# Ten matrix products of the last sequence written into the folding of a batch norm, and a load asked for earlier

## The chip, the cores and the metric

One Trainium2 chip, and one core of it. The metric is the device time of one execution in microseconds, the median of the runs. The engines are named as in the profile: PE (TensorE matmuls), PEld (its weight loads), DVE (VectorE), ACT (ScalarE), POOL (GpSimd) and SP (SyncE, which issues the DMAs here).

## What is computed

A block of two layers over 8 sequences of 512 tokens with 256 features. The change lies in the last of four parts, a product-key layer of experts. Cut to that part:

```python
def _L1_ffn_ref(x, w_q, bn_gamma, bn_beta, keys, down_embed, up_embed):   # x: normalized, (8, 512, 256)
    q = jnp.einsum('bnd,de->bne', x, w_q)                  # 2048 columns
    mean = jnp.mean(q, axis=(0, 1))
    var = jnp.var(q, axis=(0, 1))
    q = (q - mean) * jax.lax.rsqrt(var + BN_EPS) * bn_gamma + bn_beta
    q = q.reshape(b, n, 2, H, KD).transpose(2, 0, 1, 3, 4)
    sim = jnp.einsum('pbnhd,hkpd->pbnhk', q, keys)
    sx, ix = jax.lax.top_k(sim[0], TOPK)
    sy, iy = jax.lax.top_k(sim[1], TOPK)
    all_scores = (sx[..., :, None] + sy[..., None, :]).reshape(b, n, H, TOPK * TOPK)
    all_indices = (ix[..., :, None] * NUM_KEYS + iy[..., None, :]).reshape(b, n, H, TOPK * TOPK)
    scores, pk = jax.lax.top_k(all_scores, TOPK)
    indices = jnp.take_along_axis(all_indices, pk, axis=-1)
    wd = down_embed[indices]
    wu = up_embed[indices]
    h = gelu_new(jnp.einsum('bnd,bnhkd->bnhk', x, wd))
    h = jax.nn.softmax(scores, axis=-1) * h
    return jnp.einsum('bnhk,bnhkd->bnd', h, wu)
```

The three parts before it are a gated recurrence with a matrix memory, a block of attention with experts, and a cross attention. Each part is added to x with a gate.

## The kernel before

**Two phases.** `attention_phase` computes the first three parts for one sequence after another, in the order 0, 4, 1, 5, 2, 6, 3, 7. At the end of each sequence `leave(m)` stores x (`x_d`), the normalized and transposed x (`xT_d`), and adds the sequence's products of x with itself into `gacc` and its sums into `xsum`. `chosen_phase` then computes the experts' part for 32 tiles of 128 tokens.

**The products with down.** The kernel doesn't gather rows of down. It multiplies x with all 4096 rows, sequence by sequence, in `inner_products(m)`, and stores the result in `g_d` in DRAM. A sequence needs 32 products, in 16 pairs. A product is two matmuls (L285), each of two passes in the trace, into a PSUM tile `ps_hd` from a pool of two buffers, and a copy of 128x512 into one half of `raw`, on ACT (L241) or DVE (L243). A planner (`Clock`, `Room`) chooses the copy's engine by counts of its own. A pair needs its 256 KB of down (`dw`, two buffers; the load for the pair after next is asked for right after a pair) and the sequence's x (`dx`, one buffer, 512 KB, loaded once at the start of the sequence). `raw` has two buffers too; a pair's store of 512 KB to `g_d` is issued when the generator is stepped for the next pair. All these DMAs go through SP, by `send` (L138).

**How products are spread.** `inner_products` is a generator, stepped by `down_lane`. In the attention phase a scheduler steps it in between. For the last sequence, m = 7, it has to wait for `leave(7)`, so its 32 products fall in `chosen_phase`, where `late_products(n)` steps the lane until n products are written.

**An order written by hand.** On PE, DVE, ACT, POOL and SP the instructions run in the order in which the program writes them. An instruction that waits holds up whatever is behind it on its engine.

**Between the phases** stands `fold()`, which folds the batch norm into the keys. For each of 16 blocks of columns n it multiplies `wq` with `gacc` (`ps_e`, L1568), multiplies that with `wT` on DVE (`pt`, L1573), copies the mean on ACT (`mu`, L1574) and sums on ACT (L1575). Then come short instructions on DVE for the variance (L1577 to L1579), the inverse root on POOL (`inv_sqrt`, L145 and L146), and on DVE the scaling `s` (L1581), `c` (L1583, L1584) and the scaled keys `ksc` (L1586). Then, for two halves and two blocks k, 8 small products with `wT` each (`ps_w`, L1591), copied to `mat` by ACT (L1595), and for each half 8 products of `c` with the keys (L1599), which become `shift` (L1604, L1605). `ps_e`, `ps_w` and, in the attention phase, `ps_hd` share the two buffers of the pool `ps_m`. After the folding, that pool and the weights' pools are closed, and new pools take their place.

**The tile loop** runs n from -3 to 32 in four steps u. Tile t passes through it as a pipeline:

- `similar` (L1662, L1663): the similarities, from `load_tokens` (L1634, the tile's x, `xt`);
- `search` (L1677, L1679), `rank_sums`, `best_pairs`, `differences`, `chosen`, `rows_of`: the best eight twice over, on DVE and POOL;
- `turn_over` (L1778): three transposes of `mlw` on PE;
- `fetch` (L1796): the tile's `g`, 2 MB, from `g_d`; `activate` (L1800): the gelu on ACT;
- `mark_choices` (L1809 to L1830), `weigh` (`cf`, L1842), `multiply` (L1851);
- `add_up` (`acc`, L1861) and the output (`fin`, L1869), one for each tile.

The steps with n < 0 are a prologue. In it the loop also loads `up_sb` in 8 parts of 512 KB (L1916) and fetches the first three `g`. Two products of the last sequence are written in each of the 8 steps of n = -2 and n = -1, and one at the end of each n from 0 to 15:

```python
                late_products(2 if n > -3 else 0)
            elif u == 3:
                late_products(1)
```

The functions that the diff touches, with the line numbers of the profile:

Of the kernel before, what the change touches and what calls it, by code (L numbers as in the profile page):

```python
# [23 lines left out]
B, S, D = 8, 512, 256  # L24
# [61 lines left out]
def kernel(  # L86
# [28 lines left out]
    ck = Clock()  # L115
# [21 lines left out]
    def send(dst, src, after=0.0):  # L137
        nc.sync.dma_start(dst, src)  # L138
        size = 1
        for n in dst.shape:  # L140
            size *= n
        return ck.sent(size, after)
# [5 lines left out]
    def side(t):  # L148

        return ("side", t)  # L150
# [100 lines left out]
    done = {}  # L251
    dws, dw_there, raw_free = {}, [0.0, 0.0], [0.0, 0.0]

    def inner_products(m):

        b = order[m]
        xt = late.tile([P, NK, S], F32, name="dx")
        there = send(xt, xT_d[:, :, b * S : (b + 1) * S])

        def fetch(i):  # L260
            if i < M * (NJ // 2):
                dws[i] = late.tile([P, NK, 2, P], F32, name="dw", bufs=2)
                j = 2 * (i % (NJ // 2))
                dw_there[i % 2] = send(dws[i], down[:, :, j : j + 2, :])

        def store():
            i, raw, t = kept.pop()
            raw_free[i % 2] = send(
                g_d[NC * b : NC * (b + 1), :, 2 * i : 2 * i + 2, :].rearrange(
                    "c p j s -> p c (j s)"  # L270
                ),
                raw.rearrange("p c j s -> p c (j s)"), t,
            )

        if m == 0:
            fetch(0)
            fetch(1)
        kept = []
        for i in range(NJ // 2):
            yield max(there, dw_there[i % 2], raw_free[i % 2])  # L280
            raw = late.tile([P, NC, 2, P], F32, name="raw", bufs=2)
            for u in range(2):
                ps = Room([P, S], "ps_hd")
                for k in range(NK):
                    nc.tensor.matmul(  # L285
                        ps.tile, dws[m * (NJ // 2) + i][:, k, u, :], xt[:, k, :],
                        start=(k == 0), stop=(k == NK - 1),
                    )
                ps.mm(NK * S * F4)
                t = ps.copy(raw[:, :, u, :], ps.tile.rearrange("p (c s) -> p c s", c=NC))  # L290
                if u == 0:
                    yield 0.0
            kept.append((i, raw, t))
            fetch(m * (NJ // 2) + i + 2)
            yield side(t)
            store()
        done[("down", m)] = ck.pe
# [1229 lines left out]
    def lane3():  # L1527
        for m in range(M):
            yield ("rest", ("left", m))
            yield from inner_products(m)  # L1530

    down_lane = Lane(lane3())
    with tc.manual_schedule(
        engines={
            mybir.EngineType.PE, mybir.EngineType.DVE, mybir.EngineType.Activation,
            mybir.EngineType.Pool, mybir.EngineType.SP,
        }
    ):
        with ExitStack() as phase:
            attention_phase(phase, down_lane)  # L1540
        chosen_phase(ctx, tc, locals())


def chosen_phase(ctx, tc, env):
# [5 lines left out]
    ck, down_lane, inv_sqrt = (env[k] for k in ("ck", "down_lane", "inv_sqrt"))  # L1550
# [3 lines left out]
    mat = xs.tile([P, NK, 1024], F32, name="mat")  # L1554
    shift = xs.tile([P, 1024], F32R, name="shift")

    def fold():

        nc.gpsimd.memset(shift.bitcast(F32), 0.0)
        nc.vector.tensor_reduce(gacc[:, :, D], xsum, AX.X, ALU.add)  # L1560
        n_inv = 1.0 / (NT * P)
        nc.vector.tensor_scalar(gacc, gacc, n_inv, None, ALU.mult)
        e2 = wp.tile([P, 16], F32, name="e2")
        mu = wp.tile([P, 16], F32, name="mu")
        for n in range(16):
            ps = ps_m.tile([P, S], F32, name="ps_e", tag="m")
            for k in range(NK):
                nc.tensor.matmul(  # L1568
                    ps[:, : D + 1], wq[:, k, n * P : (n + 1) * P], gacc[:, k, :],
                    start=(k == 0), stop=(k == NK - 1),  # L1570
                )
            pt = fp.tile([P, D], F32, name="pt")
            nc.vector.tensor_tensor(pt, ps[:, :D], wT[:, n, :], ALU.mult)  # L1573
            nc.scalar.copy(mu[:, n : n + 1], ps[:, D : D + 1])  # L1574
            nc.scalar.activation(pt, pt, AF.Copy, accum_out=e2[:, n : n + 1])  # L1575
        s = wp.tile([P, 16], F32, name="s")
        nc.vector.tensor_tensor(s, mu, mu, ALU.mult)  # L1577
        nc.vector.tensor_tensor(s, e2, s, ALU.subtract)
        nc.vector.tensor_scalar(s, s, 0.0, None, ALU.max)  # L1579
        inv_sqrt(s, s, EPS_LN)  # L1580
        nc.vector.tensor_tensor(s, s, bn_sb[:, 0:16], ALU.mult)  # L1581
        c = wp.tile([P, 16], F32, name="c")
        nc.vector.tensor_tensor(c, mu, s, ALU.mult)  # L1583
        nc.vector.tensor_tensor(c, bn_sb[:, 16:32], c, ALU.subtract)  # L1584
        ks = wp.tile([P, 16, 64], F32, name="ksc")
        nc.vector.tensor_tensor(ks, kT, s.unsqueeze(2).to_broadcast([P, 16, 64]), ALU.mult)  # L1586
        for h in range(2):
            for k in range(NK):
                ps = ps_m.tile([P, 8, 64], F32, name="ps_w", tag="m")
                for i in range(8):  # L1590
                    nc.tensor.matmul(  # L1591
                        ps[:, i, :], wT[:, 8 * h + i, k * P : (k + 1) * P], ks[:, 8 * h + i, :],
                        start=True, stop=True,
                    )
                nc.scalar.copy(mat[:, k, 512 * h : 512 * h + 512], ps.rearrange("p i k -> p (i k)"))  # L1595
            ps = ps_m.tile([P, 8, 64], F32, name="ps_w", tag="m")
            for i in range(8):
                n = 8 * h + i
                nc.tensor.matmul(  # L1599
                    ps[0:1, i, :], c[:, n : n + 1], kT[:, n, :], start=True, stop=True  # L1600
                )
            pr = ps[0:1].rearrange("p i k -> p (i k)")
            hi = shift[0:1, 512 * h : 512 * h + 512]
            nc.scalar.copy(hi, pr)  # L1604
            nc.vector.tensor_tensor(  # L1605
                shift[32:33, 512 * h : 512 * h + 512], pr, hi.bitcast(F32), ALU.subtract
            )
# [24 lines left out]
    def load_tokens(t):  # L1632
        sims[("x", t)] = tk.tile([P, NK, P], F32, name="xt2")
        nc.sync.dma_start(sims[("x", t)], xT_d[:, :, t * P : (t + 1) * P])  # L1634

    load_tokens(0)
    fold()
    env["psum_m"].close()
    env["tail"].close()
# [4 lines left out]
    ps_o = ctx.enter_context(tc.tile_pool(name="ps_o", bufs=1, space=PSUM))  # L1644
    ps_t = ctx.enter_context(tc.tile_pool(name="ps_t", bufs=1, space=PSUM))
    env["home"][:] = [ps_s, "sim"]

    def late_products(n):

        for _ in range(n):  # L1650
            work = ck.work
            while not down_lane.over and ck.work == work:
                down_lane.step()

    def similar(t, half):
        if half == 0:
# [221 lines left out]
    for n in range(-3, NT + 1):  # L1878
        for u in range(4):
# [32 lines left out]
            if n < 0:  # L1912
                i = 4 * (n + 3) + u
                if i < 8:
                    at = slice(4 * i, 4 * i + 4)
                    nc.sync.dma_start(up_sb[:, at], up[:, at])  # L1916
                if i in (0, 5, 8):
                    fetch(len(gts))
# [3 lines that stand above are left out]
# [54 lines left out]
```

## Time and profile before

| | us |
|---|---|
| median of 3 runs | 3795.7 |
| lowest and highest run | 3791.03, 3797.01 |
| the profiled execution, its own time | 3808.9 |
| its span, first to last instruction | 3807.1 |
| end of the attention phase (last sum into `gacc`, start) | 2790.82 |
| first `ps_e` on PE | 2793.27 |
| first `ps_w` on PE | 2815.39 |
| first similarity on PE | 2834.48 |
| first product of the last sequence on PE | 2844.21 |
| first output `fin` on DVE | 2946.52 |
| last product of the last sequence on PE, start | 3341.0 |
| last output `fin` on DVE | 3803.94 |

| engine | busy us | share of the span |
|---|---|---|
| PE | 3582.4 | 94% |
| DVE | 2393.4 | 63% |
| ACT | 1706.5 | 45% |
| POOL | 742.8 | 20% |

The mean clock that was granted to TensorE is 0.952 of full speed. SP's queue between the two phases, and in the prologue, issues in this order (start in us): the store of `xT_d` at 2787.61; `xt` of tile 0 at 2790.70; one part of up at 2791.40; `g` of tile 0 at 2809.73, when the weights' pools were free; `xt` of tile 1 at 2810.12; four parts of up from 2810.69; `dx` at 2813.62; and the first `dw` of the prologue at 2847.94.

A row of the timeline or of the windows reads as follows. A timeline row has start, duration, engine, line, operation, output and inputs, shape and count, and in brackets the idle time before it and what ended that. A windows row has the stretch, its length, the busy time of PE, PEld, DVE, ACT and POOL with the number of instructions in brackets, the granted clock, the share of the DMA engines and GB/s.

### The profile page before, as it was taken

What the parts mean: (1) busy time and instruction counts of PE and PEld (TensorE: products, weight loads), DVE (VectorE), ACT (ScalarE), POOL (GpSimd) and SP (SyncE); (2) the same over time, 40 slices, a digit from 0 to 9 for tenths busy, and PEclk for the clock granted to TensorE, in tenths of its full rate; (3) what the DMA queues carried; (4) which work ended last, traced back from release to release, by engine and by line L of the source; (5) the groups of instructions that cost most, each with busy time, mean ns of one, the idle gap of its engine ahead of it and who ended that gap; (6) DMA issues with size and microseconds to landing.
All of it is one profiled execution on the core that took longest, in us unless ns stands there. A gap on an engine that the chain in (4) does not pass through costs nothing. (4 is left out here: it accounts for less than half of the span.)

```text
span 3807.1 us, 61425 instructions
## 1 busy us (share of the span) xinstructions
PE 3582.4 (94%) x24381; PEld 2005.4 (53%) x24381; DVE 2393.4 (63%) x5622; ACT 1706.5 (45%) x2383; POOL 742.8 (20%) x964
## 2 busy tenths in 40 slices
PE   9899999999999999999999999999988999998998
PEld 5544445444544544444444454355354777776777
DVE  4566466565565465556555545443337999999996
ACT  3154555454555554554555454544423333332331
POOL 2011001001001011010000101000024555555544
PEclk9799999899999999999999999998988999999999
DMA  3213213224234225223413433424333323222221
GB/s 106 89 45 122 70 56 135 70 90 147 91 104 166 79 88 165 96 94 118 161 55 112 158 106 119 135 68 135 100 125 123 113 91 122 92 85 106 80 79 58
DMA packets 235264, 395.16 MB, mean 104 GB/s; under 512 B 14048, under 2 KB 167936, under 8 KB 230624
## 3 DMA queue, kind: packets, MB, share of 16 engines
q1 hardware_dynamic: 232080, 388.83, 30.5%
q8 instruction: 192, 3.15, 0.3%
q10 hardware_dynamic: 2896, 2.40, 0.2%
q14 instruction: 96, 0.79, 0.1%
HBM read 252.62 MB, written 138.56 MB: 103 GB/s over the span
## 5 line engine op out<-in xcount | busy, mean ns | idle before, releaser
L724 DVE TENSOR_REDUCE nm<-sc 128x2 f32<-128x1024 f32 x768 | 937.7, 1222 | 795.8 <-PE sc L704 793.0
L762 ACT ACTIVATE pr<-sc 128x1024 f32<-128x1024 f32 x512 | 522.7, 1023 | 504.2 <-PE sc L704 495.7
L285 PE MATMUL ps_hd<-dx,dw 128*128 128x512 f32 x1024 | 515.0, 628 | 5.3 <-DVE pd L1003 2.4
L704 PE MATMUL sc<-ks,qs 32*128 32x512 f32 x1536 | 428.0, 523 | 62.2 <-DVE nm L724 35.2
L1861 PE MATMUL acc<-up_sb,g 128*128 128x256 f32 x2048 | 474.9, 386 | 5.6 <-DVE g L1851 3.9
L1861 PEld LDWEIGHTS acc<-up_sb,g 128*128 128x128 f32 x2048 | 380.1, 190 | 67.6 <-issue 15.8
L765 ACT ACTIVATE pr<-sc,m_off 128x1024 f32<-128x1024 f32 x256 | 283.2, 1112 | 290.2 <-PE sc L704 289.8
L704 PEld LDWEIGHTS sc<-ks,qs 32*128 32x128 f32 x1536 | 164.0, 190 | 454.1 <-issue 228.2
L704 PE MATMUL sc<-qs,ks 32*128 32x512 f32 x1536 | 388.6, 511 | 6.5 <-ACT pr L765 2.7
L1830 POOL TENSOR_TENSOR m<-m2b,wr 64x512 bf16<-64x512 bf16 x256 | 271.6, 1061 | 409.0 <-DVE m L1822 394.9
L704 PE MATMUL sc<-mx,pick_g 4*128 4x512 f32 x1536 | 309.0, 403 | 0.0
L285 PEld LDWEIGHTS ps_hd<-dx,dw 128*128 128x128 f32 x1024 | 180.9, 194 | 219.2 <-issue 191.0
L781 PE MATMUL av<-pr,va 128*32 128x512 f32 x2048 | 288.7, 637 | 2.3 <-ACT pr L762 2.3
L241 ACT COPY raw<-ps_hd 128x512 f32<-128x512 f32 x209 | 122.2, 586 | 295.3 <-PE ps_hd L285 287.0
L1800 ACT ACTIVATE g<-g 128x1024 f32<-128x1024 f32 x128 | 135.3, 1060 | 259.6 <-DMA g<-g_d 217.6
L1842 PEld LDWEIGHTS <-m 128*128 128x128 bf16 x6144 | 208.0, 98 | 36.3 <-issue 21.5
L1842 PE MATMUL cf<-m,m 128*128 128x64 bf16 x6144 | 212.8, 194 | 13.7 <-POOL m L1830 10.7
L970 POOL TENSOR_SCALAR_AFFINE_SELECT mb<-mb 128x256 f32<-128x256 f32 x116 | 47.2, 407 | 908.0 <-ACT pd L979 471.6
L348 PE MATMUL ps_up<-ones,ident 128*128 128x128 f32 x1144 | 209.2, 324 | 6.8 <-DVE dx L906 1.5
L348 PEld LDWEIGHTS ps_up<-ones,ident 128*128 128x128 f32 x1144 | 169.1, 207 | 84.0 <-issue 49.4
L145 POOL TENSOR_SCALAR ln_rs<-ln_mv 128x4 f32<-128x4 f32 x40 | 9.2, 230 | 973.9 <-DVE ln_mv L163 973.9
L1822 DVE TENSOR_TENSOR m<-m2b,wr 64x1024 bf16<-64x1024 bf16 x256 | 178.8, 699 | 8.4
(272 smaller groups left out, 5456.1 us busy)
## 6 DMA issues: line engine op xcount, KB each, us to landing
g_d<-raw SPq DMA_DIRECT2D x128, 512.0 KB
g<-g_d SPq DMA_DIRECT2D x32, 2048.0 KB
dw<-in_down SPq DMA_DIRECT2D x128, 256.0 KB
w1e<-in_w SPq DMA_DIRECT2D x32, 512.0 KB
w2e<-in_w SPq DMA_DIRECT2D x32, 512.0 KB
qs<-im_Aq SPq DMA_DIRECT2D x32, 512.0 KB
ks<-im_Ak SPq DMA_DIRECT2D x32, 512.0 KB
mb<-nM_d SPq DMA_DIRECT2D x29, 512.0 KB
```

The source lines that it names most:

```text
L285: nc.tensor.matmul(ps.tile, dws[m * (NJ // 2) + i][:, k, u, :], xt[:, k, :], start=(k == 0), stop=(k == NK - 1),)
L348: nc.tensor.matmul(ps.tile[:, :P], ident, ones, start=True, stop=True)
L704: nc.tensor.matmul(sc[:, i, :], lhs[r : r + rows], rhs[r : r + rows], start=(n == 0), stop=(n == len(terms) - 1),)
L724: nc.vector.tensor_reduce(self.nm[:, c, 2 * half : 2 * half + 2, g], sc, AX.X, ALU.max, negate=True)
L762: nc.scalar.activation(self.pr[jj], sc, AF.Exp, scale=self.scale)
L765: nc.scalar.activation(self.pr[jj], sc, AF.Exp, bias=m_off[:, col : col + 1], scale=self.scale,)
L781: nc.tensor.matmul(self.av[32 * j : 32 * j + 32, :], self.va[:, c, h * (self.hd + 1) : h * (self.hd + 1) + 32], pr[j // 2][:, j % 2, :], s ...
L1800: nc.scalar.activation(part, part, AF.Gelu_apprx_tanh)
L1822: last = nc.vector.tensor_tensor(m2[r, 0:2, :, NJ * d : NJ * d + NJ, :], m2b[r].unsqueeze(1).to_broadcast([64, 2, 8, NJ, 2]), wr[r, u, 0:2 ...
L1830: after(nc.gpsimd.tensor_tensor(m2[r, 2, :, NJ * d : NJ * d + NJ, :], m2b[r], wr[r, u, 2].unsqueeze(2).to_broadcast([64, 8, NJ, 2]), ALU.mult,
L1842: nc.tensor.matmul(cf[:, s, :], m1[:, s // 2, :, s % 2], m2[:, i, s // 2, :, s % 2], start=(i == 0), stop=(i == 2),)
L1861: nc.tensor.matmul(accs[t], gts[t][:, j, :], up_sb[:, j, :], start=(j == 0), stop=(j == NJ - 1))
```

## The change

`inner_products` notes in `done[("begun", m)]` that its x was asked for. Before `load_tokens(0)` and the folding, the lane is now stepped until the last sequence has begun, so its request for `dx` is written right behind the stores of the attention phase. `late_products` is unchanged, but stands ahead of `fold()`, which now calls it: for one product after each of the blocks n = 7, 10 and 13, for three after the inverse root has been written and before `s` is scaled, and for one after each of the four copies of `mat`. That makes ten. These are the sequence's first ten products (five pairs), with the loads of `dw` and the stores that go with them; the later calls of `late_products` are the same, so the 8 steps of the prologue write the next 16, and the last 6 follow in n = 0 to 5.

```diff
@@ -256,6 +256,7 @@
         b = order[m]
         xt = late.tile([P, NK, S], F32, name="dx")
         there = send(xt, xT_d[:, :, b * S : (b + 1) * S])
+        done[("begun", m)] = there
 
         def fetch(i):
             if i < M * (NJ // 2):
@@ -1554,6 +1555,13 @@
     mat = xs.tile([P, NK, 1024], F32, name="mat")
     shift = xs.tile([P, 1024], F32R, name="shift")
 
+    def late_products(n):
+
+        for _ in range(n):
+            work = ck.work
+            while not down_lane.over and ck.work == work:
+                down_lane.step()
+
     def fold():
 
         nc.gpsimd.memset(shift.bitcast(F32), 0.0)
@@ -1573,11 +1581,14 @@
             nc.vector.tensor_tensor(pt, ps[:, :D], wT[:, n, :], ALU.mult)
             nc.scalar.copy(mu[:, n : n + 1], ps[:, D : D + 1])
             nc.scalar.activation(pt, pt, AF.Copy, accum_out=e2[:, n : n + 1])
+            if n in (7, 10, 13):
+                late_products(1)
         s = wp.tile([P, 16], F32, name="s")
         nc.vector.tensor_tensor(s, mu, mu, ALU.mult)
         nc.vector.tensor_tensor(s, e2, s, ALU.subtract)
         nc.vector.tensor_scalar(s, s, 0.0, None, ALU.max)
         inv_sqrt(s, s, EPS_LN)
+        late_products(3)
         nc.vector.tensor_tensor(s, s, bn_sb[:, 0:16], ALU.mult)
         c = wp.tile([P, 16], F32, name="c")
         nc.vector.tensor_tensor(c, mu, s, ALU.mult)
@@ -1593,6 +1604,7 @@
                         start=True, stop=True,
                     )
                 nc.scalar.copy(mat[:, k, 512 * h : 512 * h + 512], ps.rearrange("p i k -> p (i k)"))
+                late_products(1)
             ps = ps_m.tile([P, 8, 64], F32, name="ps_w", tag="m")
             for i in range(8):
                 n = 8 * h + i
@@ -1633,6 +1645,8 @@
         sims[("x", t)] = tk.tile([P, NK, P], F32, name="xt2")
         nc.sync.dma_start(sims[("x", t)], xT_d[:, :, t * P : (t + 1) * P])
 
+    while ("begun", B - 1) not in env["done"]:
+        down_lane.step()
     load_tokens(0)
     fold()
     env["psum_m"].close()
@@ -1644,13 +1658,6 @@
     ps_o = ctx.enter_context(tc.tile_pool(name="ps_o", bufs=1, space=PSUM))
     ps_t = ctx.enter_context(tc.tile_pool(name="ps_t", bufs=1, space=PSUM))
     env["home"][:] = [ps_s, "sim"]
-
-    def late_products(n):
-
-        for _ in range(n):
...
```

## The prediction

> **What bounds the kernel now.** I read the page first, then the last thousand microseconds in windows, then the timeline of the folding, of the start of the tile loop and of SP's queue. The change touches only what follows 2790 us of a span of 3807.1, so the page's totals (PE 94%) say little here; stages do. The table by windows (span, PE, PEld, DVE, ACT, POOL busy, granted clock, DMA share, GB/s):
>
> ```profile
> 2805.00:2810.00 5.00, 3.57 (x16) 2.40 (x14) 2.38 (x8) 2.84 (x16) 0.00 (x0) 1.00 0.00 0
> 2810.00:2815.00 5.00, 0.00 (x0) 0.00 (x0) 1.53 (x5) 0.00 (x0) 3.19 (x2) 0.79 0.85 301
> 2815.00:2820.00 5.00, 4.61 (x22) 4.64 (x22) 0.25 (x1) 0.58 (x1) 0.00 (x0) 0.50 0.99 397
> 2835.00:2840.00 5.00, 5.00 (x7) 1.55 (x6) 0.39 (x3) 0.59 (x1) 0.00 (x0) 0.50 0.00 0
> 2840.00:2845.00 5.00, 5.00 (x12) 1.96 (x11) 4.68 (x45) 1.17 (x2) 0.44 (x1) 0.98 0.00 0
> ...
> 3372.60:3376.00 3.40, 0.99 (x5) 0.51 (x3) 3.33 (x7) 0.00 (x0) 2.99 (x5) 1.00 0.93 255
> 3376.20:3379.40 3.20, 3.20 (x51) 3.14 (x51) 3.12 (x8) 1.16 (x3) 0.41 (x1) 0.50 0.75 259
> ```
>
> The folding idles PE for 6.8 us from 2808.6; the clock falls to 0.50 at 2812.9 and returns only at 2840.2. The last two lines show the same in the tile loop: PE busy 0.99 us of 3.40, then one stretch at 0.50. PE's timeline of the folding:
>
> ```profile
> 2793.27 15.30 PE L1568 MATMUL ps_e<-gacc,wq 128*128 128x257 f32 x64 [2.49 <-DVE gacc L1562]
> 2815.39 7.06 PE L1591 MATMUL ps_w<-ksc,wT 128*128 128x64 f32 x32 [6.82 <-DVE ksc L1586]
> 2822.38 1.86 PE L1599 MATMUL ps_w<-kT,c 128*1 128x64 f32 x16
> 2824.18 7.09 PE L1591 MATMUL ps_w<-ksc,wT 128*128 128x64 f32 x32
> 2831.20 1.86 PE L1599 MATMUL ps_w<-kT,c 128*1 128x64 f32 x16
> ```
>
> So three stages: ps_e, bound by PE (0.956 us for each n, of which PE works about 0.9); a chain DVE, POOL (pow, 2.94 us), DVE of 6.82 us in which PE has nothing; ps_w, 17.7 us on PE at half clock. In the tile loop the output's last instruction marks a tile:
>
> ```profile
> 3339.92 0.49 DVE L1869 SCALAR_TENSOR_TENSOR fin<-acc,tg,xt 128x256 f32<-128x256 f32 x1 [0.38 <-PE acc L1861]
> 3368.01 0.48 DVE L1869 SCALAR_TENSOR_TENSOR fin<-acc,tg,xt 128x256 f32<-128x256 f32 x1 [0.37 <-PE acc L1861]
> 3397.65 0.48 DVE L1869 SCALAR_TENSOR_TENSOR fin<-acc,tg,xt 128x256 f32<-128x256 f32 x1 [1.91 <-PE acc L1861]
> 3427.38 0.48 DVE L1869 SCALAR_TENSOR_TENSOR fin<-acc,tg,xt 128x256 f32<-128x256 f32 x1 [2.01 <-PE acc L1861]
> ```
>
> All fifteen intervals up to 3368.01 are 28.09 to 28.11 us: DVE sets the pace (96 to 97% busy), and the product that each of these tiles carries costs nothing. Products end at 3341. Of the next eleven intervals (to 3686.72) six are 29.64 to 29.75, the rest 28.1. Each long one has one cold stretch: without the product PE comes 2.4 us early to the transposes (L1778), idles until mlw, the clock falls, and weigh and similar run late.
>
> **Where the cold stretches fall.** In steps of 0.2 us the falls read 3376.1, 3406.8, 3464.9, 3550.2, 3608.2 and 3666.2: distances of 9, 17, 25, 17 and 17 times 3.413 us (290.1 / 85), and the folding's fall and return lie 8 such steps apart. So the clock is judged on a fixed grid of 3.41 us. The idle stretch of a tile (fin + 5.4 to fin + 7.8) had 1.84 to 2.40 us in one grid step before every fall and at most 1.66 where none came: half a step, about 1.75 us, decides.
> The Trainium skill (TensorE: Matmul & The Clock Gate, "Part 1: The HAM clock gate") also has a free-running window, of 3413 ns. But its "HAM oscillation" section gives "no PE-idle gaps >~3.4µs" as the rule; by that a 2.4 us gap is harmless and the tile term below would be 0 instead of 6.6, for a time of 3802.4. This trace contradicts it in six tiles of eleven, and I go by the trace.
>
> **The change, part by part.** A product is four passes of L285; at full clock four products took 7.13 us (2849.99), so 1.8 each. SP and PE follow the order written.
>
> *Request for x (dx).* Moved from 2813.6 to 2790.7, ahead of tile 0's xt. Both wait for the store of xT. 512 KB on an idle queue before 2800 (share 0.00 from 2795): it is there before the first product at about 2801. xt is needed after 2834. Cost 0; if dx were late, ps_e's n = 8 would stand behind it.
>
> *Three products in ps_e.* 3 x 1.8 = 5.4 on the stage that PE bounds. Each takes over the 0.31 us for which every second n waits for mu's copy; bounds 4.5 to 5.4, I take **+5.0**. Their PSUM buffers come from ps_e's own two; the copy (ACT 0.58 or DVE 0.69) runs while the next ps_e (0.9) does, so nothing more waits.
>
> *Three products in the chain.* 5.4 us of PE work in 6.82 of idle: free for PE. But copies alternate ACT, DVE by the planner's counts, so the 4th and 6th go to DVE, and stand ahead of s times bn (L1581). The 6th ends 5.4 us after ps_e and its copy at about 6.2; s was ready at 4.95. Behind it wait both c, ksc and so all of ps_w: **+1.3** (0 if ACT takes that copy; 1.6 at most). PE then idles about 2.7 us.
>
> *Four products in ps_w.* +7.2. In return the clock: similar's four passes took 3.78 cold (2861.94) and 1.96 warm (3349.64), so 17.7 becomes 8.8. Bounds: no trace row has a warm 64-wide f32 pass; halving gives 0.11 us a pass, the nearest warm row, 128-wide transposes, 8 in 1.09, gives 0.136 and 1.8 us more; cold throughout is priced below. I take the halving, because the cold passes (0.22) follow the weight loads beside them (6.90 of 7.06). Net -1.6. The 2.7 us idle before it makes one cold step likely (0 to 3.4 us lost), +1.2: **-0.4**.
>
> *First similarities and SP.* Three at 2834.48 took 9.7 us, mostly cold; warm 7.0: -2.7. Against it: SP now meets five loads of dw and four stores in the folding, each waiting for a product or its copy, and behind them stand up, g (2 MB) and xt of tile 1, which went out at 2791 to 2813. They follow the tenth product. dw, up, g and xt are 3.0 MB; at 397 GB/s 7.6 us, with issue and landing 9.3 to 10.5. PE asks for xt of tile 1 after 0.9 (c), 1.4 (shift and the change of PSUM pools) and 4.7 (two similarities) = 7.0. Wait 2.3 to 3.5 (0 if the transfer is quicker), I take 2.5, and cold passes after it 1.0. Sum **+0.8**. Behind this wait on PE are the prologue's products, then raw's stores, g and everything up to the start of the tile loop (2895).
>
> *The prologue* keeps two products per step, of later numbers. Its own stalls begin from a product's end: dw goes out at 2847.94, then xt, up, g and the store, on which raw waits 10.84 us. They shift with it: 0 (bounds -7 to +3, the two PE waits 4.82 and 2.23 absorbed, or the queue still full of g and up).
>
> *Ten tiles lose their product.* Six are left for tiles 0 to 5; nothing is gained, as DVE sets 28.1. Twenty-one intervals instead of eleven are open to the clock. A warm tile shifts the idle stretch by 28.10 - 8 x 3.413 = 0.79 on the grid, a cold one (29.72) by 2.41. Followed from every starting phase with the 1.75 us threshold, 21 intervals give 9 to 11 cold steps and 11 give 4 to 6. I take 4 more, 4 x 1.64 = **+6.6** (3 to 6: 4.9 to 9.8).
>
> Sum: 5.0 + 1.3 - 0.4 + 0.8 + 6.6 = **+13.3 us**. The profiled execution took 3808.9 (span 3807.1, 1.8 around it), 13.2 over the median of the runs, 3795.7. 3808.9 becomes 3822.2; against the median the forecast is **3809**. Its own range adds the bounds without the prologue's: about 3800 to 3817.
>
> **Rivals.**
> *The ten tiles stay warm* (not slower). Place: the wait of L1778 for mlw. Price -6.6, so +6.7: 3802.4, within 0.2%. It decides if a tile's PE idle stays under 1.75 us in any grid step. For: five of eleven stay warm. Against: the phase moves from tile to tile, so none can stay warm for ten. 8%.
> *The prologue absorbs the folding's delay* (not slower). Price -7.0, +6.3: 3802. For: 4.82 and 2.23 us of PE waits for raw's stores. Against: those stores are behind g on SP, which is behind a product's end. It decides if PE's wait before 2862 shrinks. 13%.
> *ps_w stays cold.* Before, 17.7 us of PE nearly always busy did not raise the clock. If the 2.7 us idle starts it cold and the products do not warm it, ps_w is 17.7 + 4 x 3.6 = 32.1, +14.4 instead of -0.4, and the similarities save nothing, +2.7: 3826. Against: half of each group would be dense passes, as in the similarity that raised the clock at 2840. 7%.
> *A gain by what I do not see*, below 3788: 4%.
>
> **How the numbers follow.** The forecast has 68%. 0.2% is 7.6 us, what measurements of this kernel can tell from no change: 3788.1 to 3803.3. Slower: the forecast but its lowest part (63), the cold ps_w (7), and the upper end of the two absorbing rivals (5), 75%. Same: the rest of these, 21%. Faster 4%. The range, **3799 to 3817**, takes in the rivals near 3802 and leaves out the cold ps_w and what is below.
>
> **What would show it.** Right: the clock at 1.00 through the chain; ps_e some 20 us long; DVE's raw copy right before L1581; ps_w with products some 16 to 19 us; PE waiting for xt of tile 1; 28.1 us tiles up to the sixth, then nearly half at 29.7. Wrong: tiles 6 to 15 all at 28.1, or the tile loop starting no later than 2895.

## The result, and the profile after

| | before | after |
|---|---|---|
| median of the runs, us | 3795.29 (6 runs, 3781.37 to 3802.75) | 3819.31 (6 runs, 3805.37 to 3836.22) |
| ratio, 95% interval | | 1.0060, 1.0030 to 1.0089 |
| profiled execution: span, us | 3807.1 | 3824.2 |
| first ps_e on PE | 2793.27 | 2793.70 |
| last fin on DVE | 3803.94 | 3820.97 |

The kernel became slower. The forecast, 3809, has the right sign and about half the size; the range ended at 3817, and the median lies 2.3 us beyond it. The medians differ by 24.0 us, the two profiled spans by 17.1.

PE's timeline of the folding and behind it, after (start, duration, engine, line, operation; in brackets the wait before):

```profile
2793.70 7.65 PE L1576 MATMUL ps_e<-gacc,wq 128*128 128x257 f32 x32 [2.50 <-DVE gacc L1570]
2801.26 1.99 PE L286 MATMUL ps_hd<-dx,dw 128*128 128x512 f32 x4
2803.08 2.94 PE L1576 MATMUL ps_e<-gacc,wq 128*128 128x257 f32 x12
...
2814.15 5.42 PE L286 MATMUL ps_hd<-dx,dw 128*128 128x512 f32 x12
2822.07 2.62 PE L1602 MATMUL ps_w<-ksc,wT 128*128 128x64 f32 x16 [2.51 <-DVE ksc L1597]
2824.48 3.00 PE L286 MATMUL ps_hd<-dx,dw 128*128 128x512 f32 x4
2827.32 1.89 PE L1602 MATMUL ps_w<-ksc,wT 128*128 128x64 f32 x16
...
2841.58 1.96 PE L1669 MATMUL ps_sim<-mat,xt 128*128 128x512 f32 x4 [1.42 <-issue]
...
2850.78 3.51 PE L1669 MATMUL ps_sim<-mat,xt 128*128 128x512 f32 x4 [4.47 <-DMA xt<-xT_d]
```

The products stand where they were written: one behind each of three blocks of ps_e, three in the chain, and one behind each block of ps_w. PE's idle time before ps_w is 2.51 us instead of 6.82. The first similarity and the third read before:

```profile
2834.48 3.75 PE L1662 MATMUL ps_sim<-mat,xt 128*128 128x512 f32 x4 [1.42 <-issue]
...
2841.87 1.99 PE L1662 MATMUL ps_sim<-mat,xt 128*128 128x512 f32 x4
```

So the first now runs at full clock (1.96 instead of 3.75 us). The last line of after is the price at SP: the third, which needs xt of tile 1, waits 4.47 us, where it waited for nothing before, and then runs cold (3.51 instead of 1.99). The same stretch in windows (length, busy time of PE, PEld, DVE, ACT and POOL, granted clock, DMA share, GB/s):

```profile
2815.00:2820.00 5.00, 4.56 (x11) 1.72 (x9) 1.62 (x5) 1.02 (x4) 3.19 (x2) 1.00 0.48 148
2820.00:2825.00 5.00, 2.93 (x17) 2.88 (x18) 1.86 (x5) 0.23 (x1) 0.00 (x0) 0.82 0.54 170
2825.00:2830.00 5.00, 5.00 (x23) 3.07 (x22) 0.00 (x0) 1.53 (x3) 0.00 (x0) 0.84 0.00 0
2830.00:2835.00 5.00, 5.00 (x38) 3.49 (x37) 1.37 (x2) 1.16 (x2) 0.00 (x0) 1.00 0.49 156
...
2850.00:2855.00 5.00, 4.22 (x6) 1.66 (x7) 0.00 (x0) 0.25 (x1) 0.22 (x1) 0.66 1.03 407
```

Up to the third similarity only two single steps of the grid are cold (2823.3 to 2826.7 and 2850.5 to 2853.9, each 3.4 us), where before the clock was down for 27 us on end (2812.9 to 2840.2). DVE's timeline in the chain:

```profile
2816.16 0.69 DVE L243 COPY raw<-ps_hd 128x512 f32<-128x512 f32 x1 [0.31 <-PE ps_hd L286]
2819.60 0.69 DVE L243 COPY raw<-ps_hd 128x512 f32<-128x512 f32 x1 [2.74 <-PE ps_hd L286]
2820.21 0.17 DVE L1592 TENSOR_TENSOR s<-s,bn_sb 128x16 f32<-128x16 f32 x1
```

The sixth product's copy stands right ahead of the scaling of s. SP's queue:

```profile
2791.13 0.53 SPq L138 DMA_DIRECT2D dx<-xT_d  x1
...
2839.21 0.54 SPq L138 DMA_DIRECT2D dw<-in_down  x1
2839.80 0.60 SPq L1923 DMA_DIRECT2D up_sb<-in_up  x1
2840.45 0.42 SPq L1803 DMA_DIRECT2D g<-g_d  x1
2840.92 0.53 SPq L1646 DMA_DIRECT2D xt<-xT_d  x1
```

xt of tile 1 is issued at 2840.92, right after the tenth product's end released the dw ahead of it; before, it went out at 2810.12. And the tile loop, by its last instruction per tile:

```profile
3097.55 0.48 DVE L1876 SCALAR_TENSOR_TENSOR fin<-acc,tg,xt 128x256 f32<-128x256 f32 x1 [0.38 <-PE acc L1868]
3127.25 0.48 DVE L1876 SCALAR_TENSOR_TENSOR fin<-acc,tg,xt 128x256 f32<-128x256 f32 x1 [1.99 <-PE acc L1868]
3155.34 0.48 DVE L1876 SCALAR_TENSOR_TENSOR fin<-acc,tg,xt 128x256 f32<-128x256 f32 x1 [0.37 <-PE acc L1868]
3185.08 0.48 DVE L1876 SCALAR_TENSOR_TENSOR fin<-acc,tg,xt 128x256 f32<-128x256 f32 x1 [2.02 <-PE acc L1868]
```

3097.55 is the sixth fin. The five intervals up to it are 28.1 us; from it on, long (29.70) and short (28.09) ones nearly alternate: ten of 21 are long, where six of 26 were in all.

**Stages.** All profiled executions can be compared from the first ps_e on. The table has for each the stages in us, worked out from the starts and durations in PE's and DVE's timelines. "ps_e" is from its first start to its last end, "chain" from there to the first ps_w, "fin 1" from the first ps_e to the first fin, "tiles" from the first fin to the 27th, "long" the intervals over 29 us among these, "all" from the first ps_e to the last fin.

| kernel | first ps_e at | ps_e | chain | ps_w | fin 1 | tiles | long | all |
|---|---|---|---|---|---|---|---|---|
| before | 2793.27 | 15.30 | 6.82 | 17.67 | 153.25 | 740.20 | 6 | 1010.67 |
| after | 2793.70 | 20.61 | 7.76 | 18.08 | 163.35 | 746.69 | 10 | 1027.27 |
| again | 2757.76 | 22.16 | 7.76 | 18.11 | 165.49 | 745.03 | 9 | 1030.14 |
| after_tiles | 2787.22 | 22.00 | 7.77 | 18.09 | 165.87 | 730.44 | 0 | 1015.57 |
| after_xt1 | 2779.54 | 20.61 | 7.76 | 18.09 | 157.19 | 746.55 | 10 | 1020.97 |
| before_tiles | 2785.49 | 16.93 | 6.82 | 17.67 | 154.80 | 730.51 | 0 | 1004.82 |
| no_e | 2758.61 | 15.30 | 6.82 | 16.41 | 152.10 | 744.73 | 9 | 1016.24 |
| gap3 | 2767.38 | 15.30 | 6.82 | 9.44 | 143.11 | 740.15 | 6 | 1000.85 |
| before_fold | 2770.84 | 16.88 | 6.82 | 13.08 | 147.77 | 739.98 | 6 | 1004.96 |
| both | 2776.05 | 15.30 | 6.83 | 13.08 | 146.33 | 730.44 | 0 | 996.05 |
| gap3_timed | 2782.36 | 15.30 | 6.83 | 9.43 | 139.73 | 740.14 | 6 | 999.12 |
| gap3_tiles | 2801.73 | 15.30 | 6.82 | 9.44 | 142.08 | 730.43 | 0 | 989.71 |
| gapfill_tiles | 2783.44 | 15.30 | 6.83 | 9.43 | 142.51 | 730.45 | 0 | 990.57 |

Of the +16.6 us of after, 10.1 lie ahead of the first fin and 6.5 in the tile loop. Where ps_e takes 1.4 to 1.6 us more than its kin (again, after_tiles, before_tiles, before_fold) one cold grid step fell on its beginning; in again, in steps of 0.2 us, the clock is down from 2758.6 to 2762.0. The five intervals behind the 27th fin, which "all" holds too, take 117.2 to 117.6 us in seven of these executions and 119.2 to 119.6 in the other six, in kernels of both sorts. So differences of 2 us in "all" between single executions say little.

### The profile page after: what moved, and what is told of

The parts are those of the page before. It is cut to its first block, busy times and chain, and to the rows that moved or that the text cites. A ratio compares the mean times of both kernels' runs of the same rounds, so it can differ in the third digit from the quotient of the medians.

```text
span 3824.2 us, 61441 instructions
## 1 busy us (share of the span) xinstructions
PE 3583.1 (94%) x24381; PEld 2001.7 (52%) x24381; DVE 2397.4 (63%) x5627; ACT 1703.4 (45%) x2378; POOL 742.3 (19%) x964
## 4 chain that ended last, share of the span: by engine, by line
PE 77%; DVE 12%; ACT 4%; issue 3%; DMA 3%; POOL 2%; SPq 0%; POOLq 0%; ACTq 0%; DVEq 0%
PE sc L705 15%; PE ps_hd L286 12%; PE av L782 10%; PE acc L1868 9%; DVE nm L725 4%; PE cf L1849 4%; PE ps_up L349 3%; PE ps_sim L1669 3%; PE ps_q L573 3%; PE ps_y L1222 3%; PE ps_p L562 3%; PE ps_h L1195 2%; PE cav L1016 2%; PE csc L996 2%; DVE m L1829 1%
## 5 line engine op out<-in xcount | busy, mean ns | idle before, releaser
L241 ACT COPY raw<-ps_hd 128x512 f32<-128x512 f32 x204 | 119.2, 585 | 267.1 <-PE ps_hd L286 258.4
```

## The experiments

**again: how large is the loss?** No edit.

> The changed kernel unaltered, to size its loss. My theory (the profile's own +17.0 us is the loss: 10.5 up to the start of the tile loop, 6.5 from four more cold tiles; the +24 of the six runs is the scatter of where the clock's grid falls): ratio 1.0035 to 1.0060, 13 to 23 us slower. Rival (the typical execution loses more than the profiled one, by something the profile does not show): 1.006 or more, 24 us and up.

Ratio 1.0044, interval 1.0017 to 1.0072; medians 3815.36 (12 runs) and 3795.05, 20.3 us apart. Its profiled execution lost 19.5 us from the first ps_e on, 1.6 of them the cold step in ps_e, and yet its span was only 3791.1, because ps_e began at 2757.76. The code ahead of ps_e is the same work in the same order in every kernel here but for the request for dx, and its length ran from 2757.8 to 2801.7. So single executions scatter by some 40 us ahead of the change, and the stages tell what the runs can't. The theory's 13 to 23 us holds for the ratio; the rival's 24 and up is inside the interval still, but neither profiled execution of this kernel lost more than 19.5 from the first ps_e on.

**after_tiles: are the long tiles a matter of the clock?**

```diff
+    def keep_warm():
+        ps = ps_s.tile([P, S], F32, name="ps_warm", tag="sim")
+        for _ in range(2):
+            nc.tensor.matmul(ps, ident, mat[:, 0, 0:512], start=True, stop=True)
...
             elif u == 3:
                 late_products(1)
+                if 6 <= n < 28:
+                    keep_warm()
```

> The changed kernel, with two matmuls of 128x512 into an unread PSUM tile (1.8 us, as a product takes) at the end of each n from 6 to 27, where no product is left. Theory (those tiles are long because PE idles 2.4 us and the clock falls): every interval of fin from the sixth to the 27th is 28.1 us, no cold stretch there; the ten long ones of 29.7 go, 10 x 1.64 = 16.4 us less than the changed kernel, about 0 against before. Rival (a tile without the product's copy, loads and stores is slow for another reason, or PE's added work delays DVE): the long intervals stay, or all become longer than 28.1; 10 us or more above before.

```profile
3121.66 0.48 DVE L1881 SCALAR_TENSOR_TENSOR fin<-acc,tg,xt 128x256 f32<-128x256 f32 x1 [0.36 <-PE acc L1873]
3149.75 0.48 DVE L1881 SCALAR_TENSOR_TENSOR fin<-acc,tg,xt 128x256 f32<-128x256 f32 x1 [0.37 <-PE acc L1873]
3177.84 0.48 DVE L1881 SCALAR_TENSOR_TENSOR fin<-acc,tg,xt 128x256 f32<-128x256 f32 x1 [0.37 <-PE acc L1873]
...
3093.60:3683.50 589.90, 567.73 (x5734) 433.80 (x5733) 571.21 (x2121) 195.90 (x336) 309.55 (x379) 1.00 0.26 91
```

These are DVE's fins from the seventh on and the windows row from the sixth to the 27th. All 26 intervals are 28.09 or 28.10 us, the clock is 1.00 throughout, and the tiles take 730.44 instead of 746.69 us: 16.3 less, as expected. Ratio to before 0.9986 (0.9961 to 1.0011). The rival falls: work that nobody reads, without copies, loads or stores, does what the products did.

**before_tiles: the same on the kernel before.** The same edit with `16 <= n < 28`.

> The kernel before, with the same two matmuls at the end of each n from 16 to 27. Theory: its six intervals of 29.7 become 28.1, 6 x 1.64 = 9.8 us less (4 to 6 such tiles in a typical execution: 6.6 to 9.8), ratio 0.9974 to 0.9983. Rival: no change, within 0.1%.

The tiles take 730.51 us, 9.7 less than before. Ratio 0.9984 (0.9957 to 1.0010): right in size, but the runs alone don't settle it, and from the first ps_e on this execution gained only 5.85 us, since ps_e had a cold step (1.6) and the last five intervals took 2.3 more.

**after_xt1: what does the late xt cost?**

```diff
     load_tokens(0)
+    load_tokens(1)
...
-            if within(n + 4) and u == 1:
+            if within(n + 4) and n > -3 and u == 1:
```

> The changed kernel, with xt of tile 1 asked for right behind xt of tile 0, ahead of the folding. Theory (PE waits 4.47 us for that load and loses 1.5 us more to the cold stretch that the wait brings): PE's third similarity follows the second without a wait, the first product after it ends some 5 to 6 us earlier than in the changed kernel, and the tile loop starts as much earlier: 4 to 6 us less than the changed kernel. Rival (g and up, queued behind the folding, hold the prologue anyway): the wait is found again at raw's store before 2873, and the tile loop starts within 1.5 us of the changed kernel's.

```profile
2829.74 1.98 PE L1670 MATMUL ps_sim<-mat,xt 128*128 128x512 f32 x4
2831.65 0.50 PE L1671 MATMUL ps_sim<-shift,ones_r 64*128 64x512 f32 x1
2832.08 1.98 PE L1670 MATMUL ps_sim<-mat,xt 128*128 128x512 f32 x4
```

PE's third similarity follows the second at once. The first fin comes at 157.19 us after the first ps_e instead of 163.35: 6.2 less, a little over the expected 4 to 6. From the first similarity to the first fin it takes 109.30 us, against 115.47, 116.03 and 116.58 in after, again and after_tiles, so the gain doesn't hang on one execution. Nothing of it is given back at raw's store. Ratio 1.0019 (0.9990 to 1.0047), against 1.0044 of the unaltered kernel in again; these intervals overlap, and the price rests on the stages.

**no_e: are the products in ps_e hidden?** The two lines behind `if n in (7, 10, 13)` taken out.

> The changed kernel without the three products after n = 7, 10 and 13: seven in the folding, three of them in the chain and four in ps_w, thirteen left for the tiles n = 0 to 12. Theory (ps_e is bound by PE, and each product there costs nearly its whole 1.8 us): from the first to the end of the last ps_e 15.2 us as before, 5.3 less than in the changed kernel; chain and ps_w unchanged; the third similarity still waits some 4 us for xt of tile 1. Rival (ps_e has slack under its copies, and the products there are half hidden): 2 to 3 us less.

One execution, read by stages. ps_e takes 15.30 us, 5.31 less: three products cost nearly their whole 3 x 1.8 there. The expectation that the chain and ps_w would stay was wrong. With three products the copies go ACT, DVE, ACT, the last one no longer stands ahead of s, the chain is back at 6.82, PE idles 1.50 us instead of 2.51, and no cold step falls on ps_w: 16.41 instead of 18.08. PE's wait for xt of tile 1 is 2.95 us here, not some 4. The expectation miscounted the rest, too: nine products are left for the tiles, n = 0 to 8, and from there on nine of 18 intervals are long.

**gap3: does ps_w need products of its own?** The call behind the copy of `mat` taken out as well; only `late_products(3)` is left in the folding.

> Only the three products in the chain are left in the folding; ps_w has none. Theory (a stretch of ps_w alone, bound by loads of small weights, does not keep the clock up): the clock falls within one or two grid steps after ps_w begins, and ps_w takes 14 to 18 us. Rival (only the 6.8 us of idle brought the clock down before): the clock stays at 1.00 and ps_w takes 9 to 10.6 us.

PE's timeline and the windows of it:

```profile
2782.58 5.42 PE L286 MATMUL ps_hd<-dx,dw 128*128 128x512 f32 x12
2789.50 3.76 PE L1600 MATMUL ps_w<-ksc,wT 128*128 128x64 f32 x32 [1.50 <-DVE ksc L1595]
2793.18 1.05 PE L1608 MATMUL ps_w<-kT,c 128*1 128x64 f32 x16
2794.17 3.79 PE L1600 MATMUL ps_w<-ksc,wT 128*128 128x64 f32 x32
2797.89 1.05 PE L1608 MATMUL ps_w<-kT,c 128*1 128x64 f32 x16
```

```profile
2790.00:2795.00 5.00, 5.00 (x53) 4.82 (x52) 0.06 (x1) 1.75 (x3) 0.00 (x0) 1.00 1.03 399
2795.00:2800.00 5.00, 3.94 (x43) 3.68 (x42) 1.04 (x2) 1.75 (x3) 0.00 (x0) 1.00 0.99 398
```

My theory fell, by one execution. ps_w alone holds the full clock for its 9.44 us, and 32 passes take 3.76 us, where the same passes took 7.06 at half clock. The first fin is 10.1 us earlier than before. There is a new wait of 5.45 us for dw in the prologue (three products end in the middle of a pair, so its load is asked for behind g), and the first fin is early all the same.

**gap3_timed.** The same kernel, run twelve times.

> The kernel with only the three products in the chain, timed. Theory (ps_w holds a clock that is already up, whatever the phase of the grid, as it did in the one look): ps_w 9.4 us again, 9 to 11 us less than before from the first ps_e to the last fin, ratio 0.997 to 0.998. Rival (the one look met a lucky phase): ps_w falls to half clock within it, 14 us or more, and no gain.

ps_w 9.43, 11.6 us less than before from the first ps_e on; ratio 0.9975, 0.9947 to 1.0004, which by itself doesn't exclude no gain. The phase of the grid hardly differed: followed back in steps of 3.413 us from the next fall of the clock (2820.8 in gap3, 2838.9 here), an edge of the grid lies 0.6 us behind ps_w's start there and 0.3 us here. Two whole steps then hold nothing but ps_w, and in the third PE idles 1.1 to 1.4 us. In gap3_tiles and gapfill_tiles below the edge lies 0.6 and 0.5 us behind the start. So the rival of a lucky phase is not settled by the traces: that ps_w holds the clock was seen four times, at nearly one phase.

**before_fold: the clock without moving work.**

```diff
+    def dense(n):
+        ps = ps_m.tile([P, S], F32, name="ps_warm", tag="m")
+        for _ in range(n):
+            nc.tensor.matmul(ps, ident, wq[:, 0, 0:512], start=True, stop=True)
...
         inv_sqrt(s, s, EPS_LN)
+        dense(7)
...
                 nc.scalar.copy(mat[:, k, 512 * h : 512 * h + 512], ps.rearrange("p i k -> p (i k)"))
+                dense(1)
```

> The kernel before, with nothing moved, but seven matmuls of 128x512 into an unread PSUM tile in the chain and one after each of the four copies of mat. Theory (the folding's loss before is the clock, not a want of work): clock 1.00 from 2793 to the first similarity, ps_w with its four matmuls 12 to 13 us instead of 17.7, the first three similarities 7.0 instead of 9.7; the tile loop starts 7 to 8 us earlier, counted from the first ps_e: 0.998 of before. Rival (the prologue waits for g and up anyway): the tile loop starts less than 2 us earlier.

ps_w with its four matmuls takes 13.08 us, the first fin comes 5.5 us earlier, 7.1 if the cold step in ps_e (1.6) is taken off. The rival (under 2 us) falls. Ratio 0.9986, 0.9944 to 1.0027: four runs don't resolve it.

**both.** Both sets of unread matmuls on the kernel before.

> The kernel before with both kinds of unread matmuls: seven and four in the folding, and two at the end of each n from 16 to 27. Theory: both gains add, 7 to 8 us in the folding and 6.6 to 9.8 in the tiles: 14 to 17 us less than before, ratio 0.9955 to 0.9965. Rival (the clock's grid gives one of them back elsewhere): less than 8 us.

From the first ps_e on 996.05 us, 14.6 less than before, as expected: 6.9 ahead of the first fin, 9.8 in the tiles, less 2.1 in the last five intervals (119.28 instead of 117.22; gap3_tiles, with no cold tile either, has 117.20 there). The timed ratio missed the expectation: 0.9988, 0.9952 to 1.0023, from six runs; an interval of 0.7% can't tell 0.4% from nothing.

**gap3_tiles and gapfill_tiles: the best of both.** The three products in the chain with `keep_warm()` for `13 <= n < 28`; and seven unread matmuls in the chain, none in ps_w, with `keep_warm()` for `16 <= n < 28`.

> The same, with two unread matmuls of 128x512 at the end of each n from 13 to 27. Theory: the folding's 10 us and the tile loop's 9.7 (740.2 to 730.5 from the first to the 27th fin) add: 991 to 993 us from the first ps_e to the last fin instead of 1010.7, ratio 0.9945 to 0.996. Rival (the last five tiles, which took 2 us longer in runs without cold tiles, give more of it back): 997 or more.

> The kernel before with nothing moved: seven unread matmuls in the chain, none in ps_w, and two at the end of each n from 16 to 27. Theory (what matters in the chain is that PE is busy, not that the work is useful): ps_w 9.4 us, tile loop as in the kernel with three products moved, within 3 us of it. Rival (moving three products out of the prologue's later part is itself worth time): 4 us or more above it.

PE in gapfill_tiles:

```profile
2798.65 6.28 PE L1560 MATMUL ps_warm<-wq,ident 128*128 128x512 f32 x14
2805.57 3.76 PE L1597 MATMUL ps_w<-ksc,wT 128*128 128x64 f32 x32 [0.64 <-DVE ksc L1592]
```

gap3_tiles: 989.71 us from the first ps_e on, 21.0 less than before and 1.3 under the expected range; ratio **0.9944, 0.9914 to 0.9974**, clear of no change, and faster than both kernels. gapfill_tiles: 990.57, within 0.9 us of it; ratio 0.9964, 0.9938 to 0.9990. So it matters that PE is busy in the chain, not with what: by the stages, moving three products is worth no more than 0.9 us by itself. The two ratios' intervals overlap and don't tell them apart.

## Why the prediction was right in sign and short in size

| step | predicted | measured (after minus before) | from |
|---|---|---|---|
| dx earlier | 0 | 0: issued at 2791.13, nothing waits | SP's queue |
| three products in ps_e | +5.0 | +5.3 | after; no_e undoes it |
| three in the chain | +1.3 | +0.9 | after; no_e undoes it |
| four in ps_w, clock | -0.4 | +0.4 | 18.08 instead of 17.67 |
| first similarities and SP | +0.8 | +3.4 | first similarity to first fin, 115.47 instead of 112.04 |
| prologue | 0 | 0 | see below |
| ten tiles | +6.6 | +6.5 | ten long intervals instead of six |
| sum | +13.3 | +16.6 | |

**Right.** Every mechanism on the list is in the trace: the cold step at ps_w, the copy ahead of s, PE's wait for xt, ten tiles open to the clock. The extra cold steps of the tiles came to 4, as followed on the grid; two other executions with ten products in the folding, again and after_xt1, had 9 and 10 long intervals. That it was just 4 is in part luck, since the phase decides between 9 and 10. The prologue moved as one piece: the first dw of the prologue is issued 10.44 us later than before (2858.38) and the first fin 10.53 later.

**The step of the sum that failed** is "First similarities and SP", **+0.8**. The wait was put at 2.5 us out of a reckoned 2.3 to 3.5, and is 4.47; the cold passes behind it were put at 1.0. after_xt1 prices both together at 6.2 us, not 3.5. From dw's issue (2839.21) PE's resumption at 2850.78 is 11.6 us away, where 9.3 to 10.5 were reckoned, with 3.0 MB at 397 GB/s. In windows from 2841 to 2850.7 the rate is 311 to 393 GB/s, 355 in the mean. That is 3.4 MB, more than the 3.0 MB up to xt, so some of what was issued behind xt must have moved before PE resumed. With the wait gone the rest of the term is right: 115.47 - 6.16 is 2.7 under before's 112.04, the 2.7 us put down for warm similarities.

**ps_w** was mis-sized by 0.8. The halving of its passes was nearly right (3.76 us for 32 passes in gap3, where it gives 3.53), and the cold step that the 2.5 us of idle brought cost 1.7 (18.08 against 16.41 in no_e) instead of 1.2. Warm, ps_w with its four products took 1.26 less than before's 17.67 instead of 1.6: ps_w alone takes 9.44 in gap3 instead of 8.8, and the four products add 7.0 to it instead of 7.2.

**The rest of the miss** is in the last step, from the sum to the forecast. 16.6 us from the first ps_e on, or 17.1 of span, laid on the median gives 3812, inside the range. The six runs' median was 24.0 above before's, the twelve of again 20.3. The range was made of the terms' bounds alone, with nothing for the scatter of the part that the change doesn't touch. In the runs of after the span goes roughly with the mean granted clock, from 3834.4 at 0.951 to 3803.6 at 0.956. The traces show the same ahead of the first ps_e: the same work of PE (15485 instructions in the trace of the one, 15486 in the other's) took 2623.6 us of busy time at a mean clock of 0.96 in again and 2667.4 us at 0.94 in gap3_tiles, 43.9 of the 44.0 us between the two starts of ps_e; in all thirteen executions PE idles 131.6 to 136.0 us there. So most of the scatter is matmul time at a lower clock in the attention phase. What decides how much of it an execution gets, the grid's phase or something else, no experiment here tried.

**The rivals.** "The ten tiles stay warm" and "the prologue absorbs the delay" did not come: ten long tiles, and 10.44 became 10.53. "ps_w stays cold" did not come either, but its ground is the more instructive mistake: that a stretch of ps_w is cold before and can't raise the clock doesn't mean that it lets the clock fall (gap3). Had I seen this, the sum would have been about the same, but the four products in ps_w would have stood in it as a plain cost: 18.08 with them, 9.44 without.

## What to carry to other kernels

Ask separately what fills an idle stretch and what only adds to a busy one: of the ten products the three in PE's 6.8 us of idle were the whole gain (10.1 us to the first fin), and the other seven, with the wait and the cold steps that they brought, cost 20 (163.35 against 143.11). Work moved away from a place where it is free may have been of use there: the products in the tile loop took no time and kept the clock up, and without them nearly every second tile is 1.6 us longer. When a queue is passed, look for the small load behind the large one: 128 KB of xt behind 2 MB of g cost 6.2 us, and two lines in another place bring them back.

## What was not expected of the hardware

- ps_w's passes (128x64, each with its own weights) held a full clock but didn't raise a low one: PE was busy for 17.7 us at 0.50 in before and before_tiles, and for 9.4 us at 1.00 in gap3, gap3_timed, gap3_tiles and gapfill_tiles. They differ in PE's idle time before: 6.8 us against 1.5 or 0.64. The Trainium skill (TensorE: Matmul & The Clock Gate, "Part 1: The HAM clock gate") has the clock rise after one busy window of about 3.4 us; here four whole windows of nearly unbroken ps_w in before, and five in before_tiles, did not raise it, while similar's 512-wide passes did (the clock is back 5.7 us after the first of them in before, 4.7 in before_tiles). What would happen after a single cold step with ps_w alone behind it was not tried.
- Two unread matmuls (1.8 us of PE) in twelve tiles made the tile loop 9.7 us shorter. In the profiled executions the intervals with a product or such a filler, up to the 27th fin, are 28.08 to 28.11 us without exception.
- Code that is the same in all kernels ended between 2757.8 and 2801.7 us, 1.6%, in single executions.
